# Reordering one step of the first stage: products, refill, sums and decays of a state-space scan

## The chip, the cores and the metric

The kernel runs on one core of a Trainium2 chip. The metric is the device time of one execution in microseconds (us); smaller is better. A core has five engines that run side by side and meet through semaphores: TensorE (PE in the profile, its weight loads PEld), VectorE (DVE), ScalarE (ACT), GpSimd (POOL) and SyncE (SP), whose queue issues most DMAs.

## The reference, cut to what matters

The reference computes two layers. The first adds two branches to its input: a selective state-space block (a Mamba block) and a feed-forward block with weights and activations quantized to FP4. The second layer is attention and a two-layer local-attention block. The change touches only the first layer, and there the loop of the state-space scan:

```python
xz = jnp.einsum('bld,ed->ble', x, W_in)
x_in, z = (xz[..., :d_inner], xz[..., d_inner:])
...                                   # convolution, silu -> u; projections -> delta, B_ssm, C_ssm
def step(h, inp):
    d_t, u_t, B_t, C_t = inp
    dA = jnp.exp(d_t[:, :, None] * A[None])
    h = dA * h + (d_t * u_t)[:, :, None] * B_t[:, None, :]
    y_t = jnp.einsum('bdn,bn->bd', h, C_t)
    return (h, y_t)
...
y = ys.transpose(1, 0, 2) + D_param * u
y = y * jax.nn.silu(z)
return jnp.einsum('bld,ed->ble', y, W_out)
```

There are 8 batch rows of 512 tokens, 512 inner channels and 16 states per channel.

## The kernel before

The kernel has two stages. The second one (the second layer) is not touched, and the first (the first layer) is a loop over 256 steps. A step `g` stands for one batch row, one block of 128 channels and two of the 16 states (`at`, line 685): 8 rows x 4 blocks x 8 pairs of states. In each step the recurrence over 512 tokens is one instruction per state.

The work of the recurrence, by function:

- `fetch_c(g)` (690): a DMA that spreads two rows of C over 128 partitions into `cb`.
- `decay(g)` (695): ScalarE makes the two decays `da`, exp(delta times a), 512 wide. Six buffers.
- `inputs(g)` (703), called the refill here: TensorE makes the scan's additive inputs for two steps at once, in 16 matmuls, into `bu`. That tile takes four of the eight PSUM banks and has one buffer, so the refill for steps g+1 and g+2 has to wait until scan(g) has read `bu`. It is therefore issued in odd steps only.
- `scan(g)` (715): VectorE runs the two scans `hh<-da,bu`. Four buffers of `hh`.
- `times_c(g)` (723): GpSimd multiplies `hh` by `cb`.
- `sum_states(g)` (726), called the sum here: TensorE adds the two states into the PSUM tile `y` by eight transposing matmuls (four 128-token blocks for each state). `y` has one buffer.

All other work of the first layer is cut into generators, called strands: `head` (layer norm, input projection, convolution, `delta`), its parts (`diagonals`, `rank` to `turned`), the quantized feed-forward `ffn`, its weights `fp4_weights`, the gate `z`, `finish` (turns a finished `y` back and applies D and the gate), `output`, and `rotary_tables`. `skewed` (173) lays stages of several units over one another, one stage per step. `step()` (800) advances each active strand once, in the order of its rank, and so issues one stage of each. Strands that use PSUM share three banks, the tag "mm" of the pool `pmm0` (`MM = 3`), and `step()` counts how many are held (`held`), so a strand waits a step where no bank is left.

A stage that makes a product on TensorE often hands its eviction to `behind` (168): it is put into the list `late`, and `step()` issues that list at its end. So ScalarE's evictions come after the strands' direct ScalarE work of the step.

All engines but SyncE are wrapped in `Ordered` (45): within the first stage every engine runs its instructions in the order in which the Python code issues them. The order of calls in the loop (lines 826 to 855) is therefore the order on each engine. In an odd step TensorE gets the refill, the sum of state g-2, the strands' products, and the sum of state g-1; in an even step the strands' products (where g-1 is the first state of a block, its sum is issued at the start of the even step instead, which is the same place in TensorE's order). ScalarE gets the decays, the strands' direct work, and the list `late`. VectorE gets the scans and then the strands' operations. GpSimd gets the strands' operations and then `times_c`.

The strands that the text speaks of: `z` (740) begins three steps before the end of a block, makes `ps_z` in its second step, and in its third, an odd step, VectorE reads the bank (`z<-z,ps_z`), which frees it. `finish` (755) begins, in the kernel before, one step after the block's end. In `ffn`, `gate` and `up` (591 to 601) make `ps_gu` twice in a row for each half, and VectorE's `h<-h,ps_gu` reads it; `down` (610) makes `ps_d`; `rests` (512) makes `e` from `ps_dt`.

Of the kernel before, what the change touches and what calls it, by code (L numbers as in the profile page):

```python
# [18 lines left out]
NB, L, D = 8, 512, 256  # L19
NT = L // P  # L20
KC = D // P
DI, NS, DR = 512, 16, 16
NC = DI // P
# [35 lines left out]
def tile_kernel(ctx: ExitStack, tc: tile.TileContext, a: dict, out: bass.AP):  # L59
# [57 lines left out]
    with ExitStack() as s0:  # L117
# [567 lines left out]
        def at(g):  # L685
            b, s = divmod(g, STEPS)
            c, n = divmod(s, NS // 2)
            return b, c, 2 * n

        def fetch_c(g):  # L690
            b, c, n = at(g)
            cs[g] = rot.tile([P, 2, L], FP, tag="cb", bufs=3, name="cb")
            sp.dma_start(cs[g], made[b][2][n : n + 2, :].unsqueeze(0).to_broadcast([P, 2, L]))

        def decay(g):
            b, c, n = at(g)
            decays[g] = []
            for i in range(2):
                da = rot.tile([P, L], FP, tag="da", bufs=6, name="da")
                act.activation(da, delta[b, c], AF.Exp, scale=a_neg[:, c, n + i : n + i + 1])  # L700
                decays[g].append(da)

        def inputs(g):

            b, c, n = at(g)
            bu = spreads[g] = spreads[g + 1] = pbu.tile([P, 4, NT, P], FP, tag="bu", name="bu")
            for t in range(NT):
                for r in range(4):
                    rows = slice(r * QL, (r + 1) * QL)
                    pe.matmul(  # L710
                        bu[:, r, t, :], du[b, c][rows, t * P : (t + 1) * P],
                        diags_[b][n // 4][rows, t, :, :].rearrange("p n i -> p (n i)"), start=True, stop=True,
                    )

        def scan(g):
            hs[g] = rot.tile([P, 2, L], FP, tag="h", bufs=4, name="hh")
            bu = spreads[g].rearrange("p r t n -> p (r t n)")
            for i in range(2):
                dve.tensor_tensor_scan(
                    hs[g][:, i, :], decays[g][i], bu[:, 2 * (g % 2) + i :: 4], 0.0, ALU.mult, ALU.add  # L720
                )

        def times_c(g):
            pool.tensor_tensor(hs[g], hs[g], cs.pop(g), ALU.mult)

        def sum_states(g):
            b, c, n = at(g)
            if n == 0:
                ys[b, c] = py.tile([P, L], FP, tag="y", name="y")
            for i in range(2):  # L730

                for t in range(NT):
                    cols = slice(t * P, (t + 1) * P)
                    pe.matmul(
                        ys[b, c][:, cols], hs[g][:, i, cols], ident, is_transpose=True,
                        start=(n + i + t == 0), stop=(n + i == NS - 1 and t == NT - 1),
                    )
            del hs[g], decays[g], spreads[g]
# [36 lines left out]
        total = NB * STEPS  # L775
# [5 lines left out]
        for b in range(NB):  # L781
            g = b * STEPS
# [8 lines left out]
        def begin(strand, rank):  # L791
            urgency[strand] = rank
            active[strand] = 0, 0
            kept = sorted(active.items(), key=lambda s: urgency[s[0]])
            active.clear()
            active.update(kept)

        ranks = {output: 1, head: 3, ffn: 4, fp4_weights: 5, rotary_tables: 5}

        def step():  # L800
            brief = 0
            for s, (peak, kept, *briefly) in list(active.items()):
                if held[0] + peak <= MM:
                    held[0] += kept
                    brief += sum(briefly)
                    active[s] = next(s, None)
                    if active[s] is None:
                        del active[s]
            for f in late:
                f()  # L810
            late.clear()
            held[0] -= brief

        begin(head(0), 3)
        def able(g):
            b, c, n = at(g)
            return (b, c) in ready and len(diags_[b]) > n // 4

        while not able(0):
            step()  # L820
# [1 line left out]
            fetch_c(k)  # L822
            decay(k)
        inputs(0)
        g = summed = 0
        while g < total or active or any(s >= g for s in starts):
            clock[0] = g
            for f, *args in starts.pop(g, []):
                begin(f(*args), ranks[f])
            now = g < total  # L830
            while g + 2 < total and not able(g + 2):
                step()
            if g + 2 < total:
                fetch_c(g + 2)
            if now:
                scan(g)
            if g + 2 < total:
                decay(g + 2)
            if g % 2 and g + 1 < total:
                inputs(g + 1)  # L840
            while summed < min(g - 1, total):
                sum_states(summed)
                summed += 1
            if g % 2:
                gates = {g - (b * NC + c + 1) * (NS // 2) : (b, c) for b in range(NB) for c in range(NC)}
                for k, f in ((-3, z), (1, finish)):
                    if k in gates:
                        begin(f(*gates[k]), 0)
            step()
            if now:  # L850
                times_c(g)
            if g % 2 and 0 <= summed < min(g, total) and summed % (NS // 2):
                sum_states(summed)
                summed += 1
            g += 1


# [679 lines left out]
```

## Time and profile before

| | us |
|---|---|
| median of 3 runs | 3360.19 (3358.26 to 3360.55) |
| the profiled execution, its own time | 3363.26 |
| its span, first to last instruction | 3361.3 |
| first stage, from the first refill to the end of the scans (48 to 1345 us) | 1297 |
| granted TensorE clock, mean over the span | 0.948 |

The profile is one execution of the program, taken by the hardware profiler. The page gives busy time by engine, and the same in 40 slices of 84 us, in tenths. The waits list says which engine stood idle in front of which instruction, and what ended that wait: "PE bu <- DVE hh" means that TensorE waited in front of the refill until a scan had ended. All code of the first stage is recorded under one line (L53, the wrapper `Ordered`), so the rows are told apart by the names of their tiles. The 16 matmuls of a refill show as 32 records, the eight of a sum as eight.

### The profile page before, as it was taken

The numbers are of one execution on the slowest core, as the hardware profiler recorded it, in microseconds if no ns is written. First come the engines' busy times: TensorE is split into PE (matmuls) and PEld (weight loads), VectorE is DVE, ScalarE is ACT, GpSimd is POOL, SyncE is SP. The second block draws the span as 40 slices with busy tenths as digits, with TensorE's granted clock in tenths as the row PEclk, the third lists the DMA queues.
The fourth block names the chain that finished last, engine by engine and source line by source line (L and its number), as shares of the span: only waits on it lengthen the run. The fifth ranks groups of instructions, "written<-read, shape, count | busy, mean of one in ns | idle before, by whom it ended". The sixth has DMA issues, their size and how long they took to land.

```text
span 3361.3 us, 50387 instructions
## 1 busy us (share of the span) xinstructions
PE 2984.9 (89%) x19012; PEld 1836.9 (55%) x19012; DVE 2263.7 (67%) x4426; ACT 1562.5 (46%) x3399; POOL 1545.1 (46%) x1103
## 2 busy tenths in 40 slices
PE   5577798887888778899999999999999999999998
PEld 3455566665666566455555545545545545545545
DVE  6878787888888787556466566556557556556544
ACT  5464646474656553234244334334334434433533
POOL 2786777786868797223123123223213312312412
PEclk7778998998899998999999999999999999999999
DMA  3333333333333343210110111110110110110110
GB/s 111 111 104 108 117 104 124 119 117 117 114 120 109 118 138 118 85 50 35 46 49 35 46 54 37 48 50 32 65 34 32 65 34 32 65 33 32 59 34 7
DMA packets 93801, 244.42 MB, mean 73 GB/s; under 512 B 9848, under 2 KB 46712, under 8 KB 93560
## 3 DMA queue, kind: packets, MB, share of 16 engines
q1 hardware_dynamic: 92408, 237.01, 20.8%
q10 hardware_dynamic: 1152, 4.19, 0.3%
q8 instruction: 151, 2.47, 0.3%
q14 instruction: 90, 0.74, 0.1%
HBM read 231.48 MB, written 9.70 MB: 72 GB/s over the span
## 4 chain that ended last, share of the span: by engine, by line
PE 62%; DVE 17%; ACT 4%; issue 3%; POOL 2%; DMA 1%; DVEq 0%; POOLq 0%; ACTq 0%; SPq 0%
PE ps_qkv L1190 10%; DVE hh L53 6%; PE ps_g L1369 5%; PE ps_a L1369 4%; PE ps_wo L1333 3%; PE bu L53 3%; PE y L53 3%; PE lo L1303 3%; PE ps_y L1404 3%; PE ps_w L1387 3%; PE pt L1289 3%; PE ps_ls L1242 2%; PE ps_gu L53 2%; PE ps_st L1103 2%; DVE nm L1056 2%
## 5 line engine op out<-in xcount | busy, mean ns | idle before, releaser
L53 POOL TENSOR_TENSOR hh<-hh,cb 128x1024 f32<-128x1024 f32 x256 | 612.6, 2401 | 263.7 <-DVE hh L53 147.8
L53 DVE TENSOR_TENSOR_SCAN hh<-da,bu 128x512 f32<-128x512 f32 x512 | 592.3, 1199 | 65.3 <-PE bu L53 62.9
L53 PE MATMUL bu<-bd,du 32*128 32x128 f32 x4096 | 185.4, 328 | 253.7 <-DVE hh L53 240.5
L53 ACT ACTIVATE da<-delta,a_neg 128x512 f32<-128x512 f32 x512 | 338.4, 715 | 19.4 <-DVE hh L53 17.3
L53 PEld LDWEIGHTS bu<-bd,du 32*128 32x128 f32 x4096 | 158.3, 226 | 310.4 <-issue 207.5
L53 PE MATMUL y<-ident,hh 128*128 128x128 f32 x2048 | 315.9, 306 | 7.0 <-ACT delta L53 6.4
L1280 POOL TENSOR_TENSOR pr<-pr,lrs 128x512 f32<-128x512 f32 (+1 forms) x256 | 234.9, 934 | 177.4 <-DVE lrs L1278 137.6
L53 PEld LDWEIGHTS y<-ident,hh 128*128 128x128 f32 x2048 | 266.5, 158 | 55.7 <-issue 27.3
L1209 POOL TENSOR_TENSOR r<-r,r 128x512 f32<-128x512 f32 x128 | 163.0, 1273 | 285.4 <-DVE r L1207 242.9
L1261 ACT ACTIVATE pr<-ps_ls,nm 128x256 f32<-128x256 f32 (+1 forms) x512 | 222.0, 449 | 122.9 <-DVE nm L1255 116.7
L1205 DVE TENSOR_TENSOR r<-ps_qkv,tab 128x512 f32<-128x512 f32 x128 | 88.2, 689 | 200.1 <-ACT sq L1204 198.1
L1107 ACT ACTIVATE pt_e<-ps_st 128x512 f32<-128x512 f32 x320 | 166.8, 597 | 107.4 <-PE ps_st L1101 101.2
L945 POOL MEMSET sa<- 128x1 f32 x16 | 1.6, 99 | 449.9 <-DVE sf L1391 356.9
L1375 ACT ACTIVATE gl<-ps_g,b 128x512 f32<-128x512 f32 x96 | 65.9, 687 | 305.8 <-PE ps_g L1369 305.8
L1150 POOL TENSOR_TENSOR x1s<-x1s,bsum 128x256 f32<-128x256 f32 x32 | 23.2, 725 | 371.8 <-DVE x1s L1149 371.8
L1255 DVE CUSTOM_DVE_ANT_0 ps_ls<-ps_ls,mask 128x256 f32<-128x256 f32 (+1 forms) x512 | 184.1, 421 | 6.7 <-PE ps_ls L1242 5.8
L1369 PE MATMUL ps_g<-hn,wf 128*128 128x512 f32 x384 | 184.7, 604 | 4.0 <-DVE hn L1358 2.6
L1190 PE MATMUL ps_qkv<-wqkv,sf 128*128 128x512 f32 x384 | 182.4, 608 | 0.0
L1190 PE MATMUL ps_qkv<-wqkv,s 128*128 128x512 f32 x384 | 180.7, 606 | 0.0
L1376 DVE SCALAR_TENSOR_TENSOR ht<-ps_a,b,gl 128x512 f32<-128x512 f32 x80 | 60.0, 750 | 157.5 <-PE ps_a L1369 157.5
L1289 PE MATMUL pt<-ident,pr 128*128 128x128 f32 x896 | 131.3, 282 | 32.8 <-POOL pr L1280 28.1
L1369 PE MATMUL ps_a<-hn,wf 128*128 128x512 f32 x320 | 150.4, 592 | 0.0
(225 smaller groups left out, 6324.6 us busy)
## 6 DMA issues: line engine op xcount, KB each, us to landing
cb<-c_d SPq DMA_DIRECT2D x256, 512.0 KB, 3.7
wqkv<-in_wqkv SPq DMA_DIRECT2D x16, 1536.0 KB, 7.3
wf<-in_wf SPq DMA_DIRECT2D x16, 1408.0 KB, 6.3
wf<-in_wf SPq DMA_DIRECT2D x16, 768.0 KB, 4.7
tab<-tab SPq DMA_DIRECT2D x16, 512.0 KB, 3.5
wo<-in_wo SPq DMA_DIRECT2D x16, 512.0 KB, 3.7
xl<-in_x SPq DMA_DIRECT2D x8, 512.0 KB, 4.7
x<-in_x SPq DMA_DIRECT2D x8, 512.0 KB, 4.4
```

Source lines behind the costliest of these rows:

```text
L53: return self.tc.keep_in_program_order(getattr(self.engine, name)(*args, **kwargs))
L1107: act.activation(pt, banks[g], AF.Exp)
L1190: pe.matmul(ps, shifted(s, k, t * P, P), wqkv[:, k, i * IN : (i + 1) * IN], start=(k == 0), stop=(k == KC - 1),)
L1209: pool.tensor_tensor(r1[:, i], r1[:, i], r2, ALU.add)
L1255: last = dve.tensor_tensor_reduce(at, at, msk[:, 2 * P - nk :], -1.0, 3e38, ALU.add, ALU.min, nm[:, i : i + 1])
L1261: act.activation(pr[:, at], banks[r][:, at], AF.Exp, bias=nm[:, i : i + 1], scale=-1.0, accum_out=rs[:, i : i + 1],)
L1280: pool.tensor_tensor(ph, ph, rs.unsqueeze(2).to_broadcast([P, 2, nk]), ALU.mult)
L1289: pe.transpose(pt[:, j * P : (j + 1) * P], pr[:, j * P : (j + 1) * P], ident)
L1303: pe.matmul(o[r * LD : (r + 1) * LD, i * P : (i + 1) * P], lv[:, keys[j], h * LD : (h + 1) * LD], prts[r][:, (i * nkt + j) * P : (i * nkt ...
L1333: pe.matmul(ps, wo[:, c, m * P : (m + 1) * P], ot[:, c, :], start=(c == 0), stop=(c == IN // P - 1),)
L1369: pe.matmul(dst, wf1[:, k, off : off + P], hn[:, k, :], start=(k == 0), stop=(k == KC - 1))
L1387: pe.matmul(ps, wf2[:n, c, m * P : (m + 1) * P], ht[c][:n], start=(c == 0), stop=(c == NHC - 1),)
```

## The change

In each step the strands are now advanced right after the scan is issued, ahead of the refill. `step` takes a function `between`, which it calls after the strands' stages and ahead of the list `late`; the loop gives it the decays. The refill follows, then `times_c`, and at the end of every step the sum of state g-2; the counter `summed` goes. The start of `z` keeps its step; `finish` begins two steps after the end of its block instead of one, an even step.

```diff
-        def step():
+        def step(between=lambda: None):
             brief = 0
             for s, (peak, kept, *briefly) in list(active.items()):
...
+            between()
             for f in late:
                 f()
...
             if now:
                 scan(g)
-            if g + 2 < total:
-                decay(g + 2)
+            gates = {g - (b * NC + c + 1) * (NS // 2) : (b, c) for b in range(NB) for c in range(NC)}
+            for k, f in ((-3, z), (2, finish)):
+                if k in gates:
+                    begin(f(*gates[k]), 0)
+            step(lambda: g + 2 < total and decay(g + 2))
             if g % 2 and g + 1 < total:
                 inputs(g + 1)
-            while summed < min(g - 1, total):
-                sum_states(summed)
-                summed += 1
-            if g % 2:
-                gates = {g - (b * NC + c + 1) * (NS // 2) : (b, c) for b in range(NB) for c in range(NC)}
-                for k, f in ((-3, z), (1, finish)):
-                    if k in gates:
-                        begin(f(*gates[k]), 0)
-            step()
             if now:
                 times_c(g)
-            if g % 2 and 0 <= summed < min(g, total) and summed % (NS // 2):
-                sum_states(summed)
-                summed += 1
+            if 0 <= g - 2 < total:
+                sum_states(g - 2)
             g += 1
```

So TensorE's order becomes, in an odd step: the strands' products, the refill, the sum of state g-2; in an even step: the strands' products, the sum of state g-2. ScalarE's becomes: the strands' direct work, the decays, the list `late`. VectorE's and GpSimd's orders stay, but for `finish`, whose stages come one step later.

## The prediction

> **What bounds the kernel now.** I read first the page's busy line and its slices, then the busy time of each engine over the first stage, then the waits of TensorE and of VectorE in that stretch, then the timeline of one odd step.
>
> ```profile
> PE 2984.9 (89%) x19012; PEld 1836.9 (55%) x19012; DVE 2263.7 (67%) x4426; ACT 1562.5 (46%) x3399; POOL 1545.1 (46%) x1103
> DVE  6878787888888787556466566556557556556544
> ...
> 48.00:1345.00 1297.00, 1014.53 (x8258) 776.83 (x8251) 1072.19 (x1279) 728.64 (x1195) 987.31 (x568) 0.89 0.34 115
> ```
>
> The last line is the first stage, from its first refill (47.4 us) to its last scans: 1297 us for 256 steps, so 10.13 us for a pair of steps. Columns after the 1297.00: busy TensorE, its weight loads, VectorE, ScalarE, GpSimd, then the granted clock. VectorE has 1072.2/128 = 8.38 us of work in a pair and TensorE 1014.5/128 = 7.93. Neither is full, and they are almost equally loaded: the stage is held by what they wait for from one another. The second stage (2016 us, TensorE 97% busy) isn't touched.
>
> ```profile
> PE bu L53 <- DVE hh L53: 240.5, 90, 12.0
> ...
> PE ps_gu L53 <- DVE h L53: 1.3, 1, 1.3
> ```
>
> ```profile
> DVE hh L53 <- PE bu L53: 62.9, 59, 2.4
> DVE h L53 <- ACT h L53: 47.5, 23, 3.7
> DVE e L53 <- ACT du L53: 31.2, 20, 3.3
> DVE cv L53 <- ACT cv L53: 25.4, 15, 3.2
> DVE x L53 <- PE ps_d L53: 15.7, 14, 1.9
> DVE z L53 <- ACT z L53: 10.2, 11, 3.2
> ```
>
> These are the waits of that stretch (total, times, longest). TensorE loses 240.5 us in front of the refill, waiting for the scan that frees `bu`; it waits for almost nothing else. VectorE loses 62.9 us on the refill and 47.5+31.2+25.4+15.7+10.2 = 130.0 us on strand results that TensorE made and mostly ScalarE evicted. Both fit the order of before: in an odd step the products stand behind a refill that waits for the scan, so they reach VectorE late.
>
> ```profile
> 700.52 1.17 PE L53 MATMUL bu<-bd,du 32*128 32x128 f32 x32 [0.79 <-DVE hh L53]
> 701.29 0.69 DVE L53 SCALAR_TENSOR_TENSOR e<-du,ps_dt 128x512 f32<-128x512 f32 x1 [0.83 <-ACT du L53]
> 702.33 2.33 DVE L53 TENSOR_TENSOR_SCAN hh<-da,bu 128x512 f32<-128x512 f32 x2
> 703.64 2.86 PE L53 MATMUL ps_d<-w_d,ht 128*128 128x256 f32 x12
> 706.33 1.35 PE L53 MATMUL ps_gu<-w_g,xqt 128*128 128x352 f32 x4
> ```
>
> This is step 121 (start, duration, engine; lines between them left out). The refill for the next scan runs first, and scan 122 follows at 702.33. The product `ps_d` comes after, and by then the VectorE operation `e` of the same step, whose bank it takes, is long done. That is the second thing the order of before does, and it decides my forecast.
>
> **The change part by part.** Nothing is added or removed: 128 refills, 256 sums, 512 scans and the products remain.
>
> *Products ahead of the refill: the gain.* Products of an odd step no longer wait for the scan, the refill (185.4/128 = 1.45 us) and one sum (315.9/256 = 1.23): 2.68 us earlier. Those of an even step come one sum, 1.23 us, earlier. The five waits above average 2.07, 1.56, 1.69, 1.12 and 0.93 us, so nearly all of the 130 could go. But TensorE must still do, between two refills, two sums (2.47) and two steps of products ((1014.5-185.4-315.9)/128 = 4.01): 6.48 us. VectorE takes, from the end of a refill to the end of the next odd scan, four scans of 592.3/512 = 1.157 (4.63) and one step of strand work ((1072.2-592.3)/256 = 1.87): 6.50. They are equal, so in about every second pair the products are the longer side, and what VectorE saves it waits out in front of the refill. I credit half, 65 us; bounds 20 (TensorE longer in most pairs) and 110 (85% of the 130).
>
> *The refill behind the products: the loss.* The strands share three banks (`MM = 3`), and a product often takes the bank that a VectorE operation of the same step frees. That operation stands behind scan(g). Today the refill is already out by then. After the change the chain in an odd step is scan(g), that operation, the product, the refill (1.17), scan(g+1). Counted in the waits that the program of before carries on its products, 41 of 127 odd steps have such a product (those of `finish` not counted, since it moves to even steps). The price of one is: VectorE strand work up to the freeing operation, plus the products from there on, plus 1.17 and some 0.2 of handover, less the greater of that refill and the step's whole strand work, which would have covered it. With durations of the trace, step by step and never below zero:
> - freed by `z` (0.69): 23 steps, path 2.51 on average against 2.56 of strand work: 32 us in all
> - by `e`: 6 steps, path 4.09 (as in 121: `e` 0.69, `ps_d` 2.75, `ps_gu` 1.35 and what stands by them) against 1.32: 24 us
> - by `bd` 6 steps 8 us, by `h` 3 steps 6 us, by `cv` 3 steps 4 us
>
> Sum 74, which I round to 75. In step 121 alone, scan 122 would start near 707 instead of 702.3. Bounds: 30, if banks fall otherwise under the new order; 110, if products fed by GpSimd or ScalarE hold the refill as well.
>
> *Even steps.* The same happens in 28 even steps: TensorE arrives 1.23 us after the refill, but the freeing operation ends behind the scan, at 2.33 + about 0.7, so it idles 1.8 us: 50 us of TensorE's time. It reaches VectorE only where TensorE is the longer side by then; I take 15 (0 to 50).
>
> A rule of the Trainium skill stands behind the two losses (TensorE: Matmul & The Clock Gate, Part 2): matmuls keep program order, only weight loads are pulled ahead. The nearest row here agrees: in step 127 a weight load of `ps_gu` waits 0.24 us for `h`, and nothing behind it runs; no row here shows a refill behind such a product. If matmuls could overtake, the two losses would be nothing.
>
> *Decays behind the strands' work.* A decay is made two steps before its scan, and no wait of a scan for `da` shows: its 2 x 0.715 us stay covered, at least until ScalarE is two steps late. ScalarE is 728.6/1297 = 56% busy. The decays now stand behind operations such as `q_m`, which waits for GpSimd (2.4 us in all). The strands' direct ScalarE work comes 1.43 us earlier, in the `h` and `du` chains counted above. The 73 table loads (1283 ns) stay, since the logarithms lie between exponentials in either order. Cost 0; bounds -10 and +10.
>
> *Sums a step later, `finish` a step later.* State g-2 is now added at the end of step g. Its `hh` buffer (four) is needed by scan(g+2), two steps on; VectorE's wait for `hh` buffers shows 2.2 us today. The `cb` DMAs keep their place at the head of the step (3.7 us to land, two steps ahead), and `times_c` its place on GpSimd. The last `finish` starts at step 258 instead of 257, with no scans between: cost 0; bounds 0 and +10.
>
> *Clock.* Granted 0.89 over the stage; refill 741.17 took 1.61 us after 4.16 us of waiting, against 1.17. Idle time moves from before the refill to before products and sums; I take 0, bounds -30 and +10.
>
> The Trainium skill's rule on the clock gate (same page, Part 1) halves the clock after an idle window of about 3.4 us, and so speaks for the change. By it alone the 11% that is missing could come back: 0.11 x 1014.5 = 112 us of TensorE's time, an estimate from that rule, of which part is on the path.
>
> Sum: -65 + 75 + 15 = +25 us on the profiled execution's 3363.3, so 3388; that execution lies 3.1 above the median of 3360.2, so the forecast is 3385.
>
> **The rivals.**
>
> *Faster: TensorE's idle time is filled and banks seldom bind.* For it: 240.5 us of idle in one place, and 130 us of VectorE waits downstream. Against: equal work per pair, and the freeing operations behind the scan. Price: a gain of 110 less bank waits of 30 is -80; a gain of 90 less 45 is -45. It decides once the bank waits stay below half of what I count. Time 3280 to 3350, middle 3310.
>
> *No change.* The saved waits come back as refill waits: -75 and +75. Time 3354 to 3366.
>
> *Much slower: products fed by GpSimd hold the refill too.* `ps_i`, `ps_du` and transposes of quantized rows need GpSimd's result of the step before. GpSimd is 76% busy, and around 701 us it ran three `hh` products in a row (7.00 us), so it can be a step late. TensorE waits 9.4 us for `h` today. About 40 such products lie in odd steps; at 1 to 2 us each, +60 on top: 3445.
>
> That the change does nothing isn't possible: it reorders 127 odd steps.
>
> **How the numbers follow.** Bank waits win: 0.59 (own range 3367 to 3430). Much slower: 0.05. Faster: 0.29. No change: 0.07. A measurement of this kernel can tell about 0.2%, 6.7 us, from no change. So slower 0.64, same 0.07, faster 0.29. The range leaves out about a third of the faster case and the far end of the slowest: 3305 to 3440.
>
> **What would show it.** Right: VectorE's wait for the refill (62.9) above 110; the five strand waits (130) below 70; TensorE's wait before the refill for scans (240.5) below 120 and new waits of `ps_gu`, `ps_d`, `ps_dt` for VectorE of 50 or more; the last scan later than 1334. Wrong: the refill wait near 63 with the strand waits gone (faster), or many waits of `ps_i` and `ps_du` for GpSimd (much slower).

## The result, and the profile after

| | before | after |
|---|---|---|
| median, us | 3360.37 (4 runs) | 3405.59 (3404.55 to 3412.59, 4 runs) |
| ratio | | 1.014 [1.0122, 1.0157] |
| span of the profiled execution, us | 3361.3 | 3403.5 |
| last scan begins at, us | 1334.2 | 1373.9 |
| granted TensorE clock, mean over the span | 0.948 | 0.949 |

The change costs 45 us; the forecast was 25, with a range of 3305 to 3440. Of the 42 us by which the two spans differ, 39.7 are there when the last scan begins, so the loss lies in the first stage.

From the page of the changed kernel, the busy line and the slices of VectorE; then, from the windows, the stretch from the first refill to the last scans (length, busy TensorE, its weight loads, VectorE, ScalarE and GpSimd, then the granted clock):

```profile
PE 3009.4 (88%) x19012; PEld 1827.0 (54%) x19012; DVE 2276.0 (67%) x4426; ACT 1567.2 (46%) x3402; POOL 1544.5 (45%) x1103
DVE  6988777878787877665575466466556556556544
...
48.00:1385.00 1337.00, 1037.10 (x8257) 764.40 (x8258) 1085.19 (x1280) 735.45 (x1199) 987.39 (x567) 0.89 0.33 112
```

The stretch is 40 us longer with the same instructions at the same clock. VectorE works 13 us more in it and TensorE 23 us more. The rest of the loss is idle time, so the waits come next. First TensorE's waits of that stage (what it stood in front of, what ended it, total, times, longest; this list and the next run to 1400 us, 15 us past the stretch):

```profile
PE bu L53 <- DVE hh L53: 111.6, 58, 9.2
PE ps_gu L53 <- DVE h L53: 29.1, 13, 4.3
PE ps_i L53 <- POOL h L53: 26.4, 13, 3.3
...
PE ps_d L53 <- DVE e L53: 13.2, 4, 3.3
...
PE ps_gu L53 <- DVE u L53: 8.9, 5, 2.2
```

Before, TensorE stood idle in front of the refill for 240.5 us and in front of products that waited for VectorE for 9.5. Now it is 111.6 in front of the refill, and 111.4 in front of such products (the sum over all their rows, of which three are shown). The idle time has moved from the refill to the products. In odd steps these now run ahead of the refill; 51.5 of the 111.4 us fall in even steps, which have no refill. VectorE's waits in the same stage:

```profile
DVE hh L53 <- PE bu L53: 173.3, 76, 5.9
DVE x L53 <- PE ps_d L53: 17.8, 9, 3.9
DVE hh L53 <- ACT ps_dt L53: 10.9, 4, 4.2
DVE e L53 <- ACT du L53: 9.9, 7, 2.6
...
DVE z L53 <- ACT z L53: 5.2, 3, 3.6
...
DVE cv L53 <- ACT cv L53: 2.0, 3, 0.7
DVE h L53 <- ACT h L53: 2.0, 1, 2.0
```

The five strand waits fell from 130.0 to 17.8+9.9+5.2+2.0+2.0 = 36.9 us. The wait for the refill rose from 62.9 to 173.3. Four more scans (10.9 us) are listed under ScalarE's `ps_dt`, but in all four the refill had ended 0.16 to 0.17 us before the scan began, so they waited for the refill too. The strands' results come earlier, as the change meant, and more than all of that gain comes back in front of the scans.

One step shows how. This is step 115 of the changed kernel, from the timeline (start, duration, engine; lines between them left out):

```profile
680.95 2.27 DVE L53 TENSOR_TENSOR_SCAN hh<-da,bu 128x512 f32<-128x512 f32 x2
...
684.19 0.49 DVE L53 SCALAR_TENSOR_TENSOR h<-h,ps_gu 128x352 f32<-128x352 f32 x1
...
684.74 2.71 PE L53 MATMUL ps_gu<-w_u,xqt 128*128 128x352 f32 x4 [4.34 <-DVE h L53]
...
687.38 2.09 PE L53 MATMUL bu<-bd,du 32*128 32x128 f32 x32
...
689.61 1.22 DVE L53 TENSOR_TENSOR_SCAN hh<-da,bu 128x512 f32<-128x512 f32 x1 [4.92 <-PE bu L53]
```

The second `ps_gu` needs the bank that `h<-h,ps_gu` of the same step frees, and that operation stands behind scan 115. TensorE idles 4.34 us there with the refill queued behind the product, and scan 116 begins 6.4 us after scan 115 ended. Before the change the refill ran 0.06 us after the scan had ended, the product after it, and scan 116 began 2.6 us after scan 115. The example shows one thing more. After the 4.34 us of idle time the same product takes 2.71 us instead of 1.35 and the refill 2.09 instead of 1.17. The granted clock of the stretch from 684 to 688 us is 0.50. So a bank wait can also slow what follows it. Long waits did that before the change too: of the 22 refills that had waited more than 4 us then, 20 took over 1.6 us.

A ledger of VectorE's idle time shows whether this is the rule. I cut the stage at the scans and put each idle time into the gap behind an odd or an even scan. "Bank steps" are the odd steps in which the program of the changed kernel puts such a wait on a product: 39, or 38 of the 127 with a refill, since none follows step 255. The other odd steps are 89.

| VectorE idle, us | before | after | difference |
|---|---|---|---|
| gaps behind even scans | 101.5 | 5.7 | -96 |
| gaps behind odd scans, 38 bank steps | 27.4 | 128.7 | +101 |
| gaps behind odd scans, the other 89 | 90.3 | 111.6 | +21 |

The sum is +27, VectorE's own work from the first scan to the last is 12 longer, and the first scan begins 0.8 later: 40 us, the delay of the last scan. The bank steps alone take back all that the even gaps gave.

The trace also shows how much of this is a wait of TensorE. Ahead of the refill in 23 of the 38 bank steps TensorE stood idle, for 63 us in all, 50.5 of them until a VectorE operation ended. VectorE's idle time behind these steps rose from 14.3 to 75.2 us. In the other 15 no idle time of TensorE above 0.15 us shows between the scan and the refill, and VectorE's still rose from 13.1 to 53.5. Step 127 is one of them:

```profile
744.40 2.32 DVE L53 TENSOR_TENSOR_SCAN hh<-da,bu 128x512 f32<-128x512 f32 x2
...
746.69 2.75 PE L53 MATMUL ps_d<-w_d,ht 128*128 128x256 f32 x12
...
749.29 1.35 PE L53 MATMUL ps_gu<-w_g,xqt 128*128 128x352 f32 x4
...
750.56 1.17 PE L53 MATMUL bu<-bd,du 32*128 32x128 f32 x32
...
751.87 1.22 DVE L53 TENSOR_TENSOR_SCAN hh<-da,bu 128x512 f32<-128x512 f32 x1 [4.14 <-PE bu L53]
```

Two products without a wait take 4 us ahead of the refill. Eight of the 15 are like it and hold 16.6 of the 40.4 us. In the other seven (39, 73, 91, 123, 155, 187, 219), which hold 23.7, TensorE had waited 2.1 to 4.7 us for VectorE in front of a product of the even step before, and its work of the odd step began late. So of the 101 us some 60 lie in steps with a wait of their own, 24 behind a wait of the even step, and 17 where the products merely stand first. The other 89 odd steps divide as clearly: in 24 TensorE stood idle ahead of the refill, and VectorE's idle time rose from 29.9 to 49.9 us; in the 65 without, it stayed (60.4 and 61.7).

### The profile page after: what moved, and what is told of

Its sections match the earlier page's. It is cut to its first block, busy times and chain, and to the rows that moved or that the text cites. A ratio compares the mean times of both kernels' runs of the same rounds, so it can differ in the third digit from the quotient of the medians.

```text
span 3403.5 us, 50369 instructions
## 1 busy us (share of the span) xinstructions
PE 3009.4 (88%) x19012; PEld 1827.0 (54%) x19012; DVE 2276.0 (67%) x4426; ACT 1567.2 (46%) x3402; POOL 1544.5 (45%) x1103
## 4 chain that ended last, share of the span: by engine, by line
PE 59%; DVE 20%; ACT 5%; issue 3%; POOL 2%; DVEq 0%; ACTq 0%; POOLq 0%
PE ps_qkv L1184 10%; DVE hh L53 8%; PE ps_g L1363 5%; PE ps_a L1363 4%; PE ps_wo L1327 3%; PE lo L1297 3%; PE ps_y L1398 3%; PE bu L53 3%; PE pt L1283 3%; PE ps_w L1381 3%; PE ps_gu L53 2%; PE ps_ls L1236 2%; PE ps_d L53 2%; DVE nm L1050 2%; PE pt_qk L1175 2%
## 5 line engine op out<-in xcount | busy, mean ns | idle before, releaser
L53 DVE TENSOR_TENSOR_SCAN hh<-da,bu 128x512 f32<-128x512 f32 x512 | 593.1, 1200 | 200.4 <-PE bu L53 173.3
L53 PE MATMUL y<-ident,hh 128*128 128x128 f32 x2048 | 302.5, 296 | 17.0 <-ACT delta L53 17.0
L53 PEld LDWEIGHTS y<-ident,hh 128*128 128x128 f32 x2048 | 253.7, 153 | 66.3 <-issue 26.5
L53 PE MATMUL bu<-bd,du 32*128 32x128 f32 x4096 | 179.4, 321 | 112.5 <-DVE hh L53 111.6
L53 PEld LDWEIGHTS bu<-bd,du 32*128 32x128 f32 x4096 | 153.0, 220 | 172.8 <-issue 111.4
L1101 ACT ACTIVATE pt_e<-ps_st 128x512 f32<-128x512 f32 x320 | 166.6, 597 | 107.6 <-PE ps_st L1095 101.4
L1249 DVE CUSTOM_DVE_ANT_0 ps_ls<-ps_ls,mask 128x256 f32<-128x256 f32 (+1 forms) x512 | 183.9, 419 | 7.1 <-PE ps_ls L1236 6.2
```

The source lines that it names most:

```text
L53: return self.tc.keep_in_program_order(getattr(self.engine, name)(*args, **kwargs))
L1101: act.activation(pt, banks[g], AF.Exp)
L1249: last = dve.tensor_tensor_reduce(at, at, msk[:, 2 * P - nk :], -1.0, 3e38, ALU.add, ALU.min, nm[:, i : i + 1])
```

## The experiments

Each kernel was timed against the kernel before on the same chip. "Against before" is the difference of the two medians in us.

| kernel | ratio | against before | wait for the refill |
|---|---|---|---|
| the change | 1.0140 | +45.2 | 173.3 |
| refill first in every odd step | 0.9947 | -19.6 | 89.7 |
| refill first in the 39 bank steps | 0.9982 | -5.8 | 128.3 |
| refill first in the other odd steps | 1.0173 | +58.6 | 183.9 |
| decays first | 1.0102 | +34.1 | 189.3 |
| kernel before, decays late | 0.9986 | -5.9 | 65.0 |
| refill and decays first | 0.9933 | -24.3 | 85.5 |
| the change, two banks | 1.0219 | +72.1 | 158.2 |
| refill first, two banks | 1.0242 | +78.1 | 108.1 |
| the change, `silu` of one tensor | 1.0101 | +29.2 | |
| refill first, half the sums | 0.9971 | -10.6 | |
| refill first in bank steps, half the sums | 1.0014 | +3.3 | |
| refill first in 55 steps | 0.9905 | -30.7 | 101.4 |

### Is it the refill behind the products, or the decays?

```diff
-            step(lambda: g + 2 < total and decay(g + 2))
             if g % 2 and g + 1 < total:
                 inputs(g + 1)
+            step(lambda: g + 2 < total and decay(g + 2))
```

> The changed kernel with one part undone: in odd steps the refill stands ahead of the strands' products again (sums and finish stay late, decays stay behind the strands' direct work). Theory (bank waits: a product that takes a PSUM bank freed by a VectorE operation of the same step stands in front of the refill): the whole loss goes, 3350 to 3375; VectorE's wait for the refill falls from 173 to about 65 and the strand waits come back from 37 to about 130. Rival 1 (the loss comes from the sums and finish a step later, or from the decays): it stays at 3395 to 3415. Rival 2 (TensorE is simply fuller in front of the refill): also 3350 to 3375; it is told apart by the next two kernels.

Measured: 3343.64, ratio 0.9947 [0.9931, 0.9964]. The time is a little under the bounds. With the refill alone put back the kernel is 65 us faster than the change and faster than before. So the refill's place costs all of the loss, and something in the rest of the change is a gain. The waits are not those expected: the one for the refill is 89.7 us, and the five strand waits come back to 71.5 only.

```diff
-            step(lambda: g + 2 < total and decay(g + 2))
+            if g + 2 < total:
+                decay(g + 2)
+            step()
```

> The changed kernel with ScalarE's part undone: the decays stand ahead of the strands' work again, all else as changed. Theory: the decays are covered two steps ahead in either order, so within 7 us of the changed kernel, 3398 to 3412. Rival (late decays hold ScalarE's evictions, then banks, then the refill): 3385 or less.

Measured: 3397.33, ratio 1.0102 [1.0087, 1.0117], just under the bounds. Late decays cost some 11 us in the changed order. They are not the main cause.

### Is it the bank steps?

`banked` lists the 39 odd steps in which the program puts a bank wait on a product. The first kernel puts the refill first in these alone, the second (`g not in banked`) in the others alone.

```diff
-            if g % 2 and g + 1 < total:
+            first = g in banked
+            if first and g % 2 and g + 1 < total:
                 inputs(g + 1)
             step(lambda: g + 2 < total and decay(g + 2))
+            if not first and g % 2 and g + 1 < total:
+                inputs(g + 1)
```

> The changed kernel, but in the 39 odd steps in which a product waits for a VectorE operation of the same step the refill stands first; the other 88 keep products first. Theory (bank waits): in the trace of the changed kernel these 39 steps hold 129 us of VectorE's idle time between their scans against 27 before, so about 100 us go, and some 25 to 35 us of strand waits come back behind them: 3325 to 3350, faster than the kernel before. Rival 2 (TensorE fuller in front of the refill in every odd step): 39/127 of the loss of 45 us goes: about 3390.

Measured: 3357.44, ratio 0.9982 [0.9972, 0.9992].

> The complement: the refill stands first in the 88 odd steps without such a product, products stay first in the 39. Theory (bank waits): the loss of about 100 us in the 39 steps stays, and what the order saves in the others (66 us of strand waits less 21 to 30 us of refill waits) is given up: 3425 to 3455, slower than the changed kernel. Rival 2: 88/127 of the loss goes: about 3375.

Measured: 3421.86, ratio 1.0173 [1.0155, 1.0192].

Both times lie a few us outside their bounds, and together they split the 65 us. Products first in the 39 bank steps costs 58.6+19.6 = 78 us where the other steps have the refill first, and 45.2+5.8 = 51 where they have not. Products first in the others costs -5.8+19.6 = 14 us or gains 58.6-45.2 = 13. The bank steps carry the loss, as the theory had it, though the runs do not tell the waits in them from the products that merely stand first; by the trace the waits are the larger part. The gain that I expected of the other steps is not there.

### The parts that are not the refill

```diff
# kernel before
-        def step():
+        def step(between=lambda: None):
...
+            between()
             for f in late:
...
-            if g + 2 < total:
-                decay(g + 2)
...
-            step()
+            step(lambda: g + 2 < total and decay(g + 2))
```

> The kernel before with ScalarE's part of the change alone: the decays behind the strands' direct work. With the decays first, the changed kernel took 3397 against 3406, and the refill-first kernel with late decays was 20 us faster than before. Theory A (late decays cost in any order, since they wait behind products of GpSimd and hold the evictions): 3365 to 3380. Theory B (late decays are part of the gain of the refill-first kernel): 3340 to 3355. Theory C (of the forecast, nothing): within 7 us of 3363.

Measured: 3356.41, ratio 0.9986 [0.9975, 0.9997]. In the order of before, late decays gain 6 us, about what can be told from nothing.

```diff
# the change
-            step(lambda: g + 2 < total and decay(g + 2))
+            if g + 2 < total:
+                decay(g + 2)
             if g % 2 and g + 1 < total:
                 inputs(g + 1)
+            step()
```

> The changed kernel with refill and decays both first, so that only the sums and finish a step later remain of the change. Theory A (the sums alone give the gain of 20 us, and late decays cost about 8): 3330 to 3340. Theory B (late decays give it): 3355 to 3370. In both, the mean of VectorE's u<-u,cv stays near 1.9 us if the sums' part made it longer, and falls back to 1.2 if the decays did.

Measured: 3337.99, ratio 0.9933 [0.992, 0.9947]. What is left of the change in this kernel is the sums' place behind the products and `finish` a step later. Together they are worth 24 us; no kernel tells the two apart. The products of an odd step no longer stand behind a sum, and VectorE's five strand waits fall from 130.0 to 75.9 us:

```profile
DVE hh L53 <- PE bu L53: 85.5, 63, 2.4
DVE e L53 <- ACT du L53: 36.7, 29, 2.8
DVE x L53 <- PE ps_d L53: 21.1, 20, 3.8
...
DVE z L53 <- ACT z L53: 9.3, 6, 2.4
DVE h L53 <- ACT h L53: 8.8, 7, 1.7
```

The wait of `h` for ScalarE falls from 47.5 to 8.8 us and that of `cv` (25.4) is no longer in the list, while those of `e` and `x` rise by 5 each; the wait for the refill grows by 23. The last scan begins at 1304.6 instead of 1334.2.

### Two banks instead of three

The strands may hold only two of the three banks, so that a product seldom needs the bank that is freed last. The number of odd steps with a bank wait falls from 39 to 9, of even ones from 38 to 6. The same edit was made in the changed kernel and in the one with the refill first.

```diff
-                if held[0] + peak <= MM:
+                if held[0] + peak < MM:
```

> The changed kernel, with strands allowed to hold two of the three shared banks instead of three, so that a product usually finds a bank that was freed a step earlier: odd steps with a product that waits for VectorE of the same step fall from 39 to 9, even ones from 38 to 6. Strands are held up, so some of them are left over behind the last scan. Theory (bank waits): VectorE's wait for the refill falls from 173 to 70 to 100 us, the last scan starts 40 to 70 us earlier than in the changed kernel (1374), about 20 to 40 us are added behind it; time 3370 to 3400. Rival (TensorE fuller in front of the refill, banks or not): the wait stays above 140.

Measured: 3434.39, ratio 1.0219 [1.0203, 1.0234], with 158.2 us of waits for the refill.

> The same two banks with the refill first, as the partner of the kernel before this one. Theory (bank waits): with the waits gone from the products, it matters little where the refill stands: within 20 us of the partner, where with three banks the difference was 62. Rival: the difference stays at 50 or more.

Measured: 3440.38, ratio 1.0242 [1.0224, 1.0259]. With two banks the products stand ahead of the refill at no cost that shows: the difference of the pair is -6 us, within the noise, where with three banks it is +65. That agrees with the bank steps as the cause. The changed kernel speaks against it. TensorE's waits for VectorE in front of products fell from 111.4 to 49.2 us, but the wait for the refill was to fall below 100 and is 158.2, and the last scan was to begin 40 to 70 us earlier and begins at 1373.6 as before; in its partner it begins at 1383.1. Two banks also hold the strands up, and work is left over behind the last scan, so this pair decides little, and what these 158.2 us consist of stays open.

### Why do the other steps gain nothing?

The prediction's reason was that TensorE is the longer side in half of the pairs. If so, less work for TensorE must bring the gain out. In the next two kernels the first of a step's two states alone is summed: four of the eight transposing matmuls of each sum are left out.

```diff
-            for i in range(2):
+            for i in range(1):
...
-                        start=(n + i + t == 0), stop=(n + i == NS - 1 and t == NT - 1),
+                        start=(n + i + t == 0), stop=(n + i == NS - 2 and t == NT - 1),
```

> The refill-first kernel with half of the sums left out: only the first of a step's two states is added, 4 of 8 matmuls, about 1.1 us of TensorE less for a pair of steps. Partner of the next kernel. Theory (between two refills TensorE has as much to do as VectorE, so it counts): 3300 to 3330, against 3344. Rival (TensorE has room): within 10 us of 3344.

Measured: 3352.15, ratio 0.9971 [0.9959, 0.9983].

> The kernel with the refill first in the 39 steps with a bank wait and the products first in the other 88, with the same half of the sums left out. With all sums, products first in the 88 steps cost 12 us. Theory (they gain nothing since TensorE is the longer side between two refills, and what VectorE saves it waits out before the refill): with TensorE relieved, they gain, and this kernel is at least 5 us faster than its partner. Rival (products fed by GpSimd or ScalarE hold the refill there): still 5 to 20 us slower than its partner.

Measured: 3366.05, ratio 1.0014 [0.9999, 1.0029]. Each is about 9 us slower than its partner with whole sums, and the difference between the two, 14 us, is the same as with whole sums. TensorE did get room: its waits for a scan in front of the refill rose from 209.0 to 281.2 us and from 146.3 to 196.3. So its load is not the reason, and that step of the prediction was wrong. The relief was smaller than meant, though: up to the last scan TensorE is busy 64 and 86 us less, 0.5 and 0.7 us for a pair of steps where 1.1 was expected. The windows of the two kernels with the refill first, half the sums and then whole sums, have a second finding:

```profile
48.00:1306.00 1258.00, 914.82 (x7086) 661.31 (x7086) 1069.84 (x1255) 722.92 (x1183) 968.40 (x557) 0.85 0.35 117
```

```profile
48.00:1306.00 1258.00, 989.79 (x8195) 752.63 (x8196) 1074.02 (x1270) 729.90 (x1193) 982.20 (x563) 0.90 0.34 118
```

With 1109 matmul records fewer TensorE is busy 75 us less (a little of both because this kernel is less far at 1306 us), but its granted clock falls from 0.90 to 0.85. All its ten runs show the fall: 0.931 to 0.937 over the whole span, against 0.949 to 0.952.

What is left is that TensorE waits in the other steps too, as the 24 steps above show. In the traces I found three kinds. Steps 125, 157, 189 and 221 cost 15.9 us between the traces of "refill first in every odd step" and "refill first in the 39". I took them for bank waits, but the trace of the second shows TensorE waiting in each of them for GpSimd: 0.62 us for `du` and 2.29 for the `h` that `ps_i` turns. In eight steps TensorE waits for what ScalarE evicts late: in 121, 153, 185 and 217 a product, in 139, 171, 203 and 235 the sum that stands ahead of the products (3.1 to 4.9 us). Four more (49, 239, 249, 251) showed a longer gap. The last kernel puts the refill first in these 16 as well, 55 steps in all.

```diff
         banked = {
-            35, 39, 41, 43, 45, 47, 55, 57, 59, 63, 67, 71, 73, 75, 79, 83, 87, 91, 93, 95, 97, 107, 115,
...
+            35, 39, 41, 43, 45, 47, 49, 55, 57, 59, 63, 67, 71, 73, 75, 79,
+            83, 87, 91, 93, 95, 97, 107, 115, 119, 121, 123, 125, 127, 139, 147, 151,
+            153, 155, 157, 159, 171, 179, 183, 185, 187, 189, 191, 203, 211, 215, 217, 219,
+            221, 223, 235, 239, 249, 251, 255,
```

> The kernel with refill first in 39 steps, and in 16 more; products first in the other 72. In the traces of the refill-first kernel and of the 39-step kernel, the time from the scan of one odd step to the next differs by 16 us in steps 125, 157, 189 and 221: with the refill first in the 39, the banks are given out a little otherwise, and these four also have a product that waits for VectorE of the same step. Twelve others lose 28 us: in eight of them (121, 153, 185, 217 and 139, 171, 203, 235) products wait for what ScalarE evicts at the end of the step before. The remaining steps gain 27 us. Theory (products first gains where nothing of a product is made in the same step or late in the one before, and these 16 steps are why the 88 gained nothing): 3310 to 3332, faster than the refill-first kernel (3344). Rival (those differences are chance of one trace each, and products first gains nothing in any step): 3338 to 3360.

Measured: 3331.09, ratio 0.9905 [0.9887, 0.9923]. This is the fastest version: 31 us below the kernel before and 76 below the change. The edit to 16 steps took 25 us off, and in the odd steps left (73 with a refill) products first is a gain: 11 us against the kernel with the refill first in all. The 16 were picked from traces of these same kernels; what each of the three kinds is worth by itself was not measured.

### Why does VectorE work 13 us more?

By operation and shape, the row that grew most (calls, then total and mean in ns; the mean was 1162 before):

```profile
L53 DVE SCALAR_TENSOR_TENSOR u<-u,cv 128x512 f32<-128x512 f32 x28 | 55.3, 1974 | 0.0
```

That is 23 us more, partly offset elsewhere. It does not come with the loss: in the kernel with refill and decays first, which keeps only the sums' and `finish`'s new places and is faster than before, the mean is 1884. The timeline of the changed kernel shows where it comes from:

```profile
666.46 2.36 POOL L53 TENSOR_TENSOR hh<-hh,cb 128x1024 f32<-128x1024 f32 x1 [0.30 <-DVE hh L53]
666.73 2.64 DVE L53 SCALAR_TENSOR_TENSOR u<-u,cv 128x512 f32<-128x512 f32 x1
669.29 0.51 DVE L53 TENSOR_TENSOR h<-h,ps_gu 128x352 f32<-128x352 f32 x1
```

GpSimd's product starts 0.27 us earlier and ends at 668.82; `u<-u,cv` ends 0.55 us after that, and by itself it takes 0.66. The same holds for 24 of the 28: each ends 0.55 us after a GpSimd instruction, and the other four take 0.66. It looks as if it waited. The next kernel leaves out the multiplication by `cv`, so that the operation reads one tensor instead of two.

```diff
-                dve.scalar_tensor_tensor(u_[b][c], u_[b][c], 1.0, cv, ALU.add, ALU.mult)
+                dve.tensor_scalar(u_[b][c], u_[b][c], 1.0, None, ALU.add)
```

> The changed kernel with one VectorE operation made cheaper: the last step of silu (u<-u,cv, 28 in the stretch) only adds 1 to one tensor, the product with cv is left out. In the changed kernel that operation takes 0.66 us alone and up to 3.4 us where GpSimd works on two tensors in SBUF beside it, 1.97 on average against 1.16 in the kernel before, 23 us more in all. Theory (VectorE's operations on two SBUF tensors wait for GpSimd, and this is a part of the loss of 45 us): the operation falls to 0.7 us or less whatever GpSimd does, and the time by 15 to 35 us, to 3370 to 3390. Rival (that time is covered by the wait for the refill): within 7 us of 3405.

Measured: 3391.94, ratio 1.0101 [1.0079, 1.0124], above the bounds. The row became:

```profile
L53 DVE TENSOR_SCALAR u<-u 128x512 f32<-128x512 f32 x28 | 42.6, 1523 | 0.0
```

The one-tensor form takes 0.39 us at best and up to 2.54, and 24 of the 28 end 0.28 to 0.29 us after a GpSimd instruction, so it waits as well; my expectation that it would take the same whatever GpSimd does was wrong. The kernel is 16 us faster than the change, where the row gives 28 x (1.974-1.523) = 12.6: this time of VectorE is on the path.

The Trainium skill (SBUF — State Buffer, Who interferes with whom) describes a port pair that VectorE and GpSimd share as an exclusive lock: a VectorE operation with two SBUF inputs beside a GpSimd instruction that reads SBUF, or one in a two-port mode such as `tensor_scalar` can enter, contends for it, and the one that issues second blocks until the other has ended. The rows here agree for both forms (0.66 to 3.40 us and 0.39 to 2.54).

## Why the prediction was right, and where it was off

**Direction and mechanism: right.** The signs it named are all there: the wait for the refill 173.3 (above 110), the strand waits 36.9 (below 70), TensorE's wait for scans 111.6 (below 120), products that wait for VectorE 111.4 (50 or more), the last scan at 1373.9 (after 1334). By the rule on program order no matmul should overtake; step 115 shows just that, a refill behind a product that waits 4.34 us.

**The refill behind the products, +75: the size about right, the mechanism in part.** Products first in the bank steps cost 51 and 78 us in the two comparisons. The program carries 39 such odd steps, where I counted 41, and 38 even ones instead of 28. But in 15 of the 38 with a refill no wait of TensorE shows ahead of it, and they hold 40 of the 101 us of VectorE's idle time: 24 of them behind a wait of the even step before, and 17 where the products alone, once ahead of the refill, were the price. The example was wrong: in the changed kernel the banks fall otherwise, and step 121 holds no such wait. Scan 122 came 2.21 us late, not 4.7, behind a refill that followed two products without a pause and had ended 0.17 us before:

```profile
719.23 2.33 DVE L53 TENSOR_TENSOR_SCAN hh<-da,bu 128x512 f32<-128x512 f32 x2 [2.21 <-ACT ps_dt L53]
```

The list of steps taken from the program of before was thus a good count and a bad map. The price also left out that TensorE can be slower behind a wait (2.71 for 1.35 us in step 115).

**The gain of products first, -65: the step that failed.** The strand waits went even further than I credited (-93 us), but what is next late was mis-sized: in the steps without a bank wait the order is worth between -13 and +14 us, not -65. "What VectorE saves it waits out in front of refill in every second pair" holds as to the place, but not for the reason given. Halving the sums changed nothing in it. The trace and the kernel with 55 steps point to waits for GpSimd and ScalarE, which in the new order hold the refill, and that kernel shows that the steps left gain 11 us.

**Sums and `finish` a step later, 0 (bounds 0 and +10): wrong sign.** They gain 24 us. I priced the sums' buffers, and counted the 1.23 us by which TensorE's products come earlier under the first term alone, which fell together with the refill. These two are the part of the change that works. Which of them does it, and what they are worth with the products first, was not run.

**Decays, 0 (bounds -10 and +10).** +11 us in the changed order, +5 with the refill first (within the noise), -6 in the order of before. I left out that the cover of an operation depends on the order around it. The table loads rose from 73 to 76; I had them unchanged.

**Even steps, +15 (0 to 50).** TensorE's waits for VectorE in even steps are 51.5 us, as the 50 of the prediction. What of them reaches VectorE was not told apart by a kernel. VectorE's idle time behind even scans fell by 96 us, so a cost comes up only in the odd gaps: the 24 us of the seven bank steps above are the part that the trace shows.

**The clock, 0: right.** The granted clock over the stage is 0.89 before and after. TensorE's idle time did not vanish, it moved, so nothing of the 112 us that the rule allowed came back.

**The rivals.** "Faster" failed at its own point of decision: bank waits did not stay below half of what I counted. "Much slower" needed products that wait for GpSimd; these rose from 12.2 to 34.2 us, in the right place but less than the 60 it asked for.

The sum by what was measured: +65 for the refill's place (51 to 78 of it in bank steps), -24 for the sums and `finish`, +5 for the decays with the refill first. That is the way from the kernel before to the change in three steps, so it adds up to its 45 by itself; what it tells is the size of each. That the forecast of 25 came as near as it did is partly luck: the gain of 65 that did not come was partly made up by the 24 of the sums and `finish`, which I had at nothing.

## What to carry to other kernels

On an engine that runs in order, put first the instruction that releases the bottleneck, and behind it what may wait for the bottleneck's own current step or is merely long; where only some steps have such waits, choose the order step by step, as the version with 55 steps does. A wait that is taken away is worth only what the next late thing leaves of it, so follow each of them to the next wait of the engine that sets the end, and count for every product which buffer it takes and who frees it. When several things are moved at once, price each move by itself: here those that I had priced at nothing gained 24 us, and the main one lost 65.

## What the runs showed of the hardware

- Two VectorE operations whose tensors all lie in SBUF waited for GpSimd's running instruction: with two tensors read (0.66 to 3.40 us, the long ones ending 0.55 after GpSimd's) and with one (0.39 to 2.54, ending 0.28 after). Operations with a PSUM input (`h<-h,ps_gu`, 0.49 to 0.52) and a reduction over SBUF (`q_rows<-h`, 0.85 to 0.89) kept their times. So reordering a step on TensorE also changed VectorE's durations, by where they fell beside GpSimd.
- Fewer matmuls brought no time: with half of the sums' matmuls left out the granted clock fell from 0.90 to 0.85 and the kernel was 9 us slower. That the clock is what took the saving is not shown.
- A wait of 4.34 us on TensorE was followed by a product and a refill at about half their speed (2.71 for 1.35 us, 2.09 for 1.17), with a granted clock of 0.50 from 684 to 688 us.
